# Seven of eight experts' weights fetched at the start, three of them into the attention's query and key tiles

## The chip, the cores and the metric

The kernel runs on one core of a Trainium2 chip. The metric is the time of one execution on the device in microseconds (us). The core has a tensor engine (PE in the profile; PEld are its weight loads), a vector engine (DVE), a scalar engine (ACT), GpSimd (POOL) and a sync engine (SP). Each works through its own queue of instructions in order. SP issues most of the transfers from DRAM to the on-chip memory, and POOL issues the indirect ones, in which a table of row numbers says where each row goes. A transfer runs by itself once it is issued, on 16 DMA engines.

## What is computed

Two layers on 2048 tokens of 128 channels in float32. The first has a mixture of eight experts, attention with 16 heads, and the same mixture once more; the second has a channel mix, a gated long convolution and the channel mix again. The part that matters here is the mixture:

```python
def _L0_ffn_ref(s, W_in, in_norm_w, Wr, expert_bias, Wg, Wu, Wd, enorm_w, out_norm_w, W_out):
    h = rmsnorm(x @ W_in.T, in_norm_w)
    logits = h @ Wr.T
    _, idx = jax.lax.top_k(logits + expert_bias, TOP_K)          # 2 of 8 experts for each token
    gates = ...                                                  # softmax over the two chosen logits
    for e in range(Wg.shape[0]):
        gate = jax.nn.silu(h @ Wg[e].T)
        up = h @ Wu[e].T
        oe = rmsnorm(gate * up @ Wd[e].T, enorm_w[e])
        out = out + gates[:, e:e + 1] * oe
    s_hat = rmsnorm(out, out_norm_w) @ W_out.T

x = x + 0.5 * _L0_ffn_ref(_layernorm(x), ...)
x = x + _L0_attn_ref(_layernorm(x), ...)
x = x + 0.5 * _L0_ffn_ref(_layernorm(x), ...)
```

Each expert has three matrices of 128 x 512. Together with its norm weights they make 1664 numbers in each of 128 partitions (WALL), 832 KB.

## The kernel before

**Dispatch.** The tokens come in 16 tiles of 128, four to a part (EARLY). `dispatch` normalises a part, takes its two best experts for each token and computes the token's place in the list of that expert in DRAM (`hss`). POOL then writes the rows there, one indirect transfer for each tile and choice (L470). The four parts are staggered, so the scatters of one part run beside the arithmetic of the next.

**Blocks.** An expert works on blocks of rows from its list. A general block (numbers below NT = 24) holds 256 rows (15 of them, NPAIR) or 128 (9, NSING). Which expert and which rows it has is only known at run time: `table` computes that on DVE in steps, and SP reads the result into registers before it can issue the fetches.

**Early blocks.** Eight blocks, one for each expert (numbers NT to NT + 7), take the first 128 rows of that expert's list. They need no table and don't wait for the whole dispatch, only for the first six tiles (LEAD). `leading` sets them up. Their rows are fetched by `read` (L550) once the scatters of these six tiles have landed. They go into tiles that attention will later use for its values (`vs`, 512 x 4 floats a partition each). Their outputs go there too. Where an expert has fewer than 128 rows by then, masks make the block's output go nowhere, and the general blocks cover these rows.

**Order of the work.** In `experts`, `work` runs over the early blocks, then over TURNS. Turn i does on the tensor engine: the gate product of block i (`pg`, L732), the transposition of the next block's rows (`pht`, L719), the up product (`pu`, L732) and the down product of the block before (`py`, L755). Between `up` and `down` stands a piece of other work, among them the steps of the table: the last and longest (`named` with `bounded`, L632 to L664) is the piece of turn 4. `down` ends with the square sums on ACT (L772), the product with the norm weights on DVE (L773) and the scatter of the output rows on POOL (L779). Each of `py` and `pht` has one PSUM bank (tags `sb` and `sa`). After `down`, SP is given the fetches of turn i + 3: `fetch_rows` (L713) and `fetch_weights` (L705, and L527 for an early block).

**Weights.** All weight tiles come from one pool with four buffers (tag `w`). Before the dispatch begins, `first_experts` issues the fetches of experts 0 to 3 (L527). Expert 4's fetch is issued in turn 1, after the down product of expert 0 has released its buffer, and so on: expert e + 4 after expert e. A fetch waits in SP's queue until DVE has done the L773 of the block that used the buffer last, and what stands behind it in SP's queue waits as well.

**The zero fill.** Behind each list there must be rows of zeros. `zeros` writes them with one indirect transfer on POOL (L506) whose source is `blank`, the first 16 * ROW = 2064 columns of the first query and key tile, cleared by DVE at the very start (L949).

**The query and key tiles.** `qks` are two tiles of 4096 floats a partition, queries in the first half and keys in the second. Until attention they are only used as said. Pieces of turns 14 to 17 clear the query halves and set the key halves on POOL (L962, L966).

Of the kernel before, what the change touches and what calls it, by code (L numbers as in the profile page):

```python
# [10 lines left out]
F32 = mybir.dt.float32  # L11
# [5 lines left out]
P = 128  # L17
# [15 lines left out]
ROW = D + 1  # L33
# [5 lines left out]
NT = NPAIR + NSING  # L39
# [19 lines left out]
WALL = 3 * DFF + D  # L59
# [14 lines left out]
def macaron_kernel(ctx: ExitStack, tc: tile.TileContext, a: dict, out: bass.AP):  # L74
# [11 lines left out]
    def bank(name, tag=None):  # L86

        if tag is None or tag == "side":
            tags = ("sa", "sb", "px", "py", "pz") if tag is None else turn["side"]
            tag = tags[turn["bank"] % len(tags)]  # L90
            turn["bank"] += 1
        if tag[0] == "p":
            return bank_pair(name, tag)[:, 0, :]
        return psum.tile([P, 512], F32, tag=tag, name=name)
# [90 lines left out]
    def both(*pieces):  # L185
        def run():
            for piece in pieces:
                piece()

        return run  # L190
# [301 lines left out]
    def counts(f):  # L492
        pc = bank(f"pcnt_{f}", "sb")[:, 0:E]
        nc.tensor.matmul(pc, ones, ahead[:, NCH * TPC, :], start=True, stop=True)
        return pc

    def zeros(pc, mp):


        at = mp.tile([P, E], F32, tag="zat", name="zat", bufs=1)  # L500
        nc.vector.tensor_mul(at, pc, owner)
        row = mp.tile([P, 1], F32, tag="zsum", name="zsum", bufs=1)
        nc.vector.tensor_reduce(row, at, AX.X, ALU.add)
        word = mp.tile([P, 1], I32, tag="zword", name="zword", bufs=1)
        nc.vector.scalar_tensor_tensor(word, row, float(ROW), zrow, ALU.mult, ALU.add)
        ins = nc.gpsimd.indirect_dma_start(  # L506
            out=hss[0].rearrange("n w -> (n w)").unsqueeze(1),
            out_offset=bass.IndirectOffsetOnAxis(ap=word, axis=0),
            in_=blank[0],
            in_offset=None,  # L510
        )
        tc.declare_no_dep(ins.ins, group="hs0", reason="rows of their own")
        tc.add_to_no_dep_group("hs0", ins.ins)
        tc.declare_no_dep(ins.ins, group="lead", reason="full blocks, or not used")
        tc.keep_in_program_order(ins)

    def leading(gp, mp, rows, yrows):

        lead = {"w": {}, "hst": {}, "yrow": {}}
        flags = gp.tile([P, 3, E], F32, tag="lflags", name="lflags", bufs=1)  # L520
        masks = gp.tile([P, 3, E], I32, tag="lmasks", name="lmasks", bufs=1)
        idx = gp.tile([P, E], I32, tag="lidx", name="lidx", bufs=1)
        lead["taken"], lead["base"], lead["masks"], lead["idx"] = flags[:, 0], flags[:, 1], masks, idx

        def weights(e):
            lead["w"][NT + e] = mp.tile([P, WALL], F32, tag="w", name=f"w_lead_{e}", bufs=4)
            nc.sync.dma_start(lead["w"][NT + e], a["wall"][e, :, :])  # L527

        def flagged():


            pc = bank("plead", "sb")[:, 0:E]
            nc.tensor.matmul(pc, ones, ahead[:, LEAD, :], start=True, stop=True)
            full = float(P)
            nc.vector.scalar_tensor_tensor(flags[:, 2], pc, full, base, ALU.is_ge, ALU.mult)
            nc.vector.tensor_scalar(masks[:, 2], flags[:, 2], 1.0, None, ALU.max)
            nc.vector.tensor_scalar(flags[:, 0], pc, full, full, ALU.is_ge, ALU.mult)
            nc.vector.tensor_scalar(masks[:, 0], pc, full, float(FAR - 1), ALU.is_ge, ALU.mult)
            nc.vector.tensor_scalar(masks[:, 1], pc, full, float(FAR), ALU.is_lt, ALU.mult)
            nc.vector.tensor_add(flags[:, 1], flags[:, 0], base)  # L540

        def read():
            SP = mybir.EngineType.SP
            first = [
                nc.values_load(masks[0:1, 2, e : e + 1], engines=[SP], min_val=1, max_val=HS_ROWS - TT)
                for e in range(E)
            ]
            for e, row in enumerate(first):
                hst = rows[:, e * ROW : e * ROW + ROW].unsqueeze(1)
                ins = nc.sync.dma_start(  # L550
                    hst, hss[0][bass.ds(row, P), :].rearrange("(s p) c -> p s c", p=P)
                )
                tc.add_to_no_dep_group("lead", ins.ins)
                lead["hst"][NT + e] = hst
                lead["yrow"][NT + e] = yrows[:, e * ROW : e * ROW + ROW].unsqueeze(1)

        return lead, weights, flagged, read

    def table(f, pc, mp, lead=None, scratch=None):
# [115 lines left out]
    def weigh_up(f, mp):  # L675

        g = mp.tile([P, NCH * TPC, 2], F32, tag="gates", name=f"gates_{f}", bufs=1)
        mx = mp.tile([P, NCH * TPC], F32, tag="gmx", name=f"gmx_{f}", bufs=1)
        nc.vector.tensor_reduce(mx, lsel, AX.X, ALU.max)
        nc.vector.tensor_sub(g, lsel, bc_last(mx, 2))  # L680
        nc.scalar.activation(g, g, AF.Exp)
        nc.vector.tensor_reduce(mx, g, AX.X, ALU.add)
        nc.vector.reciprocal(mx, mx)
        nc.vector.tensor_mul(g, g, bc_last(mx, 2))
        return g
# [204 lines left out]
    def stagger(chunks, lag):  # L890

        n = len(chunks[0])
        for s in range(lag * (len(chunks) - 1) + n):
            for c, stages in enumerate(chunks):
                if 0 <= s - lag * c < n:
                    stages[s - lag * c]()
# [1 line left out]

    def first_experts(parts, gp, pieces, heads_):

        with tc.tile_pool(name="moe0", bufs=2, reuse_waits="tile") as mp:
            flat = [t.rearrange("p t h d -> p (t h d)") for t in heads_]
            lead, lead["weights"], flagged, read = leading(gp, mp, *flat)
            for e in range(4):
                lead["weights"](e)
            found = {}

            def counted():  # L910
                found["pc"] = counts(0)
                zeros(found["pc"], gp)

            i = LEAD // TPC
            parts[i][-2] = both(parts[i][-2], flagged)
            rows = parts[i][-1]
            parts[i][-1] = both(
                partial(rows, range(LEAD % TPC)), read, partial(rows, range(LEAD % TPC, TPC))
            )
            decays = decay_pieces()  # L920
            parts[-1][4] = both(parts[-1][4], decays[0])
            parts[-1][-1] = both(counted, parts[-1][-1])
            stagger(parts, 4)
            tab, far, steps = table(0, found["pc"], gp, lead, flat[0][:, E * ROW :])
            steps[0]()
            steps = [*steps[1:5], both(*steps[5:7])]
            steps += [lambda: None] * (E - len(steps))
            experts(0, tab, far, y2s[0], mp, steps + pieces, lead)
        return weigh_up(0, gp), decays[1:]
# [15 lines left out]
    def heads(hp):  # L945
        qks = [hp.tile([P, 2, 4, CT], F32, tag=f"qk{i}", name=f"qk{i}") for i in range(2)]
# [3 lines left out]
        vs = [hp.tile([P, TPC, H, 32], F32, tag=f"v{i}", name=f"v{i}") for i in range(2)]  # L950
# [398 lines left out]
                    for step in places_[s, "b"]:  # L1349
                        step()  # L1350

        return constant_pieces, attention, vs


    def tail(gates, y2):
# [223 lines left out]
    with tc.manual_schedule(engines={EN.PE, EN.DVE, EN.Activation, EN.SP}):  # L1579
        with tc.tile_pool(name="rows0", bufs=2) as gp:  # L1580
            with tc.tile_pool(name="heads", bufs=1, reuse_waits="tile") as hp:
                constant_pieces, attention, vs = heads(hp)
                fold_in()
                parts = [[*dispatch(0, i, EARLY, gp)] for i in range(len(EARLY))]
                early = filter_pieces()
                idle = [fold_out, fold_mu, *constant_pieces()]
                idle += [lambda: None] * (len(early) - len(idle))
                gates, decays = first_experts(parts, gp, [both(*two) for two in zip(early, idle)], vs)
                mixed = combined(0, gates, y2s[0], gp)
                attention(mixed, [dispatch(1, i, LATE, gp) for i in range(len(LATE))], decays)  # L1590
            gates = second_experts(gp)
            banks.close()
            tail(gates, y2s[1])
# [137 lines left out]
```

## Time and profile before

| | us |
|---|---|
| median of three runs | 597.49 (595.13 to 599.95) |
| the profiled execution | 594.65 |
| its span, first to last instruction | 592.9 |

| stretch of the profile, us | what runs | tensor engine busy, us | mean clock granted to it | DMA share |
|---|---|---|---|---|
| 0 to 16 | constants, inputs, four weight fetches; dispatch of the first part | 10.07 of 16 | 0.93 | 0.85 |
| 16 to 41.5 | the rest of the dispatch | 10.10 of 25.5 | 0.50 | 0.42 |
| 41.5 to 53.5 | early blocks of experts 0 to 3 | 11.96 of 12 | 0.87 | 0.36 |
| 53.5 to 66 | early blocks of experts 4 and 5, and the start of 6 | 7.70 of 12.5 | 0.86 | 0.99 |
| 66 to 72 | early blocks of experts 6 and 7 | 5.74 of 6 | 1.00 | 0.89 |
| 72 to 158 | general blocks | 82.11 of 86 | 1.00 | 0.58 |
| 158 to 375 | combination, attention, second dispatch | 193.97 of 217 | 0.99 | 0.27 |
| 375 to 470 | second mixture | 88.83 of 95 | 0.98 | 0.70 |

The rest of the span is the combination and the second layer. The clock is that which the throttle granted, as a share of full speed. The DMA share is the mean busy share of the 16 DMA engines. Over the whole span the tensor engine is busy for 519.3 us (88%), DVE for 356.6, ACT for 272.7 and POOL for 193.3.

A line of the timeline gives the start in us, the duration, the engine, the line of the kernel, the operation and its tiles, and in brackets the time that the engine sat idle before it with what ended the wait. A number of instructions (x8) can be merged in one line.

### The profile page before, as it was taken

What the parts mean: (1) busy time and instruction counts of PE and PEld (TensorE: products, weight loads), DVE (VectorE), ACT (ScalarE), POOL (GpSimd) and SP (SyncE); (2) the same over time, 40 slices, a digit from 0 to 9 for tenths busy, and PEclk for the clock granted to TensorE, in tenths of its full rate; (3) what the DMA queues carried; (4) which work ended last, traced back from release to release, by engine and by line L of the source; (5) the groups of instructions that cost most, each with busy time, mean ns of one, the idle gap of its engine ahead of it and who ended that gap; (6) DMA issues with size and microseconds to landing.
All of it is one profiled execution on the core that took longest, in us unless ns stands there. A gap on an engine that the chain in (4) does not pass through costs nothing. (4 is left out here: it accounts for less than half of the span.)

```text
span 592.9 us, 11265 instructions
## 1 busy us (share of the span) xinstructions
PE 519.3 (88%) x3921; PEld 397.7 (67%) x3921; DVE 356.6 (60%) x1114; ACT 272.7 (46%) x669; POOL 193.3 (33%) x201
## 2 busy tenths in 40 slices
PE   5458899999779989998898888699999989789996
PEld 5347898898536555565465554379999974568874
DVE  5766454564335766767778866634444432868775
ACT  4563232223334556566766654123233223884365
POOL 0677445753331201011003447313333335420110
PEclk9559899999999999999999999999999999989999
DMA  8536956666040355064030001368767725000002
GB/s 303 204 86 205 317 202 217 176 202 211 24 108 28 46 146 212 1 190 170 25 48 20 28 28 46 113 207 246 231 208 237 228 76 144 2 1 1 0 2 71
DMA packets 37598, 74.30 MB, mean 125 GB/s; under 512 B 4571, under 2 KB 26882, under 8 KB 36256
## 3 DMA queue, kind: packets, MB, share of 16 engines
q1 hardware_dynamic: 33040, 64.00, 35.4%
q0 software_dynamic: 4496, 9.52, 4.6%
q8 instruction: 33, 0.54, 0.4%
q14 instruction: 29, 0.24, 0.1%
HBM read 52.66 MB, written 21.38 MB: 125 GB/s over the span
## 5 line engine op out<-in xcount | busy, mean ns | idle before, releaser
L779 POOL DMA_INDIRECT y<-yrow_f,idx_f x64 | 62.9, 984 | 106.5 <-issue 56.6
L1160 ACT ACTIVATE es<-ps 128x1024 f32<-128x1024 f32 x64 | 65.3, 1021 | 52.5 <-PE ps L1123 30.9
L1143 DVE TENSOR_REDUCE m<-pm 128x4 f32<-128x1024 f32 x64 | 77.5, 1220 | 12.3 <-PE pm L1106 12.3
L1123 PE MATMUL ps<-qa,qk 32*128 32x256 f32 x512 | 72.7, 401 | 11.9 <-ACT es L1160 9.6
L470 POOL DMA_INDIRECT hs<-hrow,posi_f x64 | 61.8, 965 | 53.9 <-issue 23.9
L748 DVE TENSOR_TENSOR hg_f<-pu_f,sg_f 128x1024 f32<-128x1024 f32 (+1 forms) x45 | 45.5, 1011 | 51.0 <-PE pu_f L732 51.0
L1106 PE MATMUL pm<-qk 32*128 32x256 f32 x512 | 73.2, 400 | 0.6 <-ACT qk L1053 0.6
L732 PE MATMUL pg_f<-ht_f,w_f 128*128 128x256 f32 (+1 forms) x296 | 63.6, 359 | 3.0 <-DMA w_f<-in_wall_dram 1.6
L755 PE MATMUL py_f<-w_f,hg_f 128*128 128x128 f32 x512 | 63.8, 276 | 2.0 <-DVE idx_f L776 1.2
L755 PEld LDWEIGHTS py_f<-w_f,hg_f 128*128 128x128 f32 x512 | 61.7, 192 | 3.7 <-DVE yrow_f L773 2.3
L772 ACT ACTIVATE ysq_f<-py_f 128x128 f32<-128x128 f32 x72 | 19.4, 274 | 96.9 <-PE py_f L755 89.1
L1123 PEld LDWEIGHTS ps<-qa,qk 32*128 32x128 f32 x512 | 43.6, 184 | 30.0 <-ACT es L1160 22.4
L741 ACT ACTIVATE sg_f<-pg_f 128x1024 f32<-128x1024 f32 (+1 forms) x45 | 38.4, 853 | 53.3 <-PE pg_f L732 51.7
L732 PE MATMUL pu_f<-ht_f,w_f 128*128 128x256 f32 (+1 forms) x296 | 61.7, 351 | 0.0
L732 PEld LDWEIGHTS pg_f<-ht_f,w_f 128*128 128x128 f32 x296 | 49.7, 194 | 8.5 <-DVE hg_f L748 2.2
L732 PEld LDWEIGHTS pu_f<-ht_f,w_f 128*128 128x128 f32 x296 | 48.7, 191 | 5.0
L1106 PEld LDWEIGHTS pm<-qk 32*128 32x128 f32 x512 | 44.5, 184 | 2.5 <-issue 1.5
L773 DVE TENSOR_TENSOR yrow_f<-py_f,w_f 128x256 f32<-128x256 f32 (+1 forms) x37 | 14.4, 389 | 38.0 <-ACT ysq_f L772 38.0
L1170 PE MATMUL po<-es,v 128*32 128x256 f32 x512 | 34.9, 391 | 0.0
L171 POOL TENSOR_TENSOR cf_f<-cf_f,mhalf 128x8 f32<-128x8 f32 (+1 forms) x9 | 13.5, 1502 | 64.3 <-DVE cf_f L844 63.5
L724 DVE TENSOR_SCALAR ht_f<-pht_f,pack 128x256 f32<-128x256 f32 (+1 forms) x37 | 16.5, 446 | 23.7 <-PE pht_f L719 23.7
L1155 DVE TENSOR_TENSOR qa<-pmt,qk 128x256 f32<-128x256 f32 x32 | 13.5, 422 | 25.8 <-PE pmt L1149 24.3
(306 smaller groups left out, 926.4 us busy)
## 6 DMA issues: line engine op xcount, KB each, us to landing
w_f<-in_wall_dram SPq DMA_DIRECT2D x36, 832.0 KB, 4.9
hs<-blank SPq DMA_DIRECT2D x8, 1032.0 KB, 15.1
w_lead<-in_wall_dram SPq DMA_DIRECT2D x8, 832.0 KB, 7.8
y_f<-y SPq DMA_DIRECT2D x14, 258.0 KB, 5.0
hst_f<-hs SPq DMA_DIRECT2D x27, 129.0 KB, 3.0
pack<-in_pack_dram SPq DMA_DIRECT2D x1, 1729.0 KB, 8.6
heads<-qkc SPq DMA_DIRECT2D x3, 512.0 KB, 2.6
qk<-heads SPq DMA_DIRECT2D x12, 128.0 KB
```

What stands on the lines that cost most here:

```text
L470: ins = nc.gpsimd.indirect_dma_start(out=hss[f], out_offset=bass.IndirectOffsetOnAxis(ap=st["posi"][:, t, k : k + 1], axis=0), in_=hrow[:, ...
L732: nc.tensor.matmul(ph[:, k, :], w[t][:, o + k * P : o + k * P + P], ht[t], start=True, stop=True)
L741: nc.scalar.activation(sg, pg, AF.Silu)
L748: nc.vector.tensor_mul(hg[t], pu, sg)
L755: nc.tensor.matmul(py[:, s, :], hg[t][:, k, ts(s, P)], w[t][:, 2 * DFF + k * D : 2 * DFF + k * D + D], start=(k == 0), stop=(k == NFC - 1),)
L772: nc.scalar.activation(sq[:, s], py[:, s], AF.Square, accum_out=yrow[:, s, D : D + 1])
L779: ins = nc.gpsimd.indirect_dma_start(out=y2, out_offset=bass.IndirectOffsetOnAxis(ap=idx[:, s : s + 1], axis=0), in_=yrow[:, s, :], in_off ...
L1106: nc.tensor.matmul(sc[:, jj, i, :], qs[c][r, g, col + i * P : col + (i + 1) * P], ks[c][r, g, col : col + S], start=True, stop=True,)
L1123: nc.tensor.matmul(sc[:, jj, i, :], ks[c][r, g, col + i * P : col + (i + 1) * P], tops[s][r, :], start=True, stop=True,)
L1143: nc.vector.tensor_reduce(m, sc, AX.X, ALU.max, negate=True)
L1160: nc.scalar.activation(es, sc, AF.Exp, scale=scale)
L1170: nc.tensor.matmul(po[32 * j : 32 * j + 32, :], vs[c][:, (b % 2) * 2 + i, (g % 2) * (H // 2) + (g // 2) * 4 + j, :], ess[s, j // 2][:, j % ...
```

## The change

The weights of the early blocks get places of their own for three experts: expert 0 and expert 1 in the second query and key tile, one behind the other (2 x 1664 of its 4096 columns), and expert 2 in the first, behind the 2064 columns that hold the zeros. The four buffers of the pool then hold experts 3 to 6. Seven fetches are issued before the dispatch and not four. Expert 7 takes the buffer that expert 3 releases, in turn 4 as before, and the general blocks follow as before.

```diff
-    def leading(gp, mp, rows, yrows):
+    def leading(gp, mp, homes, rows, yrows):
...
         def weights(e):
-            lead["w"][NT + e] = mp.tile([P, WALL], F32, tag="w", name=f"w_lead_{e}", bufs=4)
+            if e in homes:
+                lead["w"][NT + e] = homes[e]
+            else:
+                lead["w"][NT + e] = mp.tile([P, WALL], F32, tag="w", name=f"w_lead_{e}", bufs=4)
             nc.sync.dma_start(lead["w"][NT + e], a["wall"][e, :, :])
...
-    def first_experts(parts, gp, pieces, heads_):
+    def first_experts(parts, gp, pieces, qks, vs):
...
-            flat = [t.rearrange("p t h d -> p (t h d)") for t in heads_]
-            lead, lead["weights"], flagged, read = leading(gp, mp, *flat)
-            for e in range(4):
+            wide = [t.rearrange("p i g s -> p (i g s)") for t in qks]
+            flat = [t.rearrange("p t h d -> p (t h d)") for t in vs]
+            homes = {0: wide[1][:, 0:WALL], 1: wide[1][:, WALL : 2 * WALL]}
+            homes[2] = wide[0][:, 16 * ROW : 16 * ROW + WALL]
+            lead, lead["weights"], flagged, read = leading(gp, mp, homes, *flat)
+            for e in range(7):
                 lead["weights"](e)
...
-        return constant_pieces, attention, vs
+        return constant_pieces, attention, qks, vs
...
-                constant_pieces, attention, vs = heads(hp)
+                constant_pieces, attention, qks, vs = heads(hp)
...
-                gates, decays = first_experts(parts, gp, [both(*two) for two in zip(early, idle)], vs)
+                gates, decays = first_experts(parts, gp, [both(*two) for two in zip(early, idle)], qks, vs)
```

## The prediction

> **What bounds the kernel now.** The page's second part comes first, to find stages in which the engines are starved:
>
> ```profile
> span 592.9 us, 11265 instructions
> ...
> PEclk9559899999999999999999999999999999989999
> DMA  8536956666040355064030001368767725000002
> ```
>
> A slice is 14.8 us. DMA is busy in slice 0, falls to 5 and 3 tenths in slices 1 and 2, and stands at 9 in slice 4 (59 to 74 us), just where the granted clock dips to 8: the transfers are bunched, and TensorE is waiting beside them. The chain of waits doesn't reach so far back (it begins at 374 us), so the stage of the eight early blocks is read from the timeline of TensorE, 50 to 72 us (these are lines of one answer; every left-hand number is a start):
>
> ```profile
> 55.52 1.13 PE L732 MATMUL pg_f<-ht_f,w_lead 128*128 128x128 f32 x8 [2.03 <-DMA w_lead<-in_wall_dram]
> ...
> 61.33 1.77 PE L732 MATMUL pg_f<-ht_f,w_lead 128*128 128x128 f32 x8 [2.78 <-DMA w_lead<-in_wall_dram]
> ...
> 65.82 1.06 PE L732 MATMUL pg_f<-ht_f,w_lead 128*128 128x128 f32 x8
> ...
> 68.61 1.06 PE L732 MATMUL pg_f<-ht_f,w_lead 128*128 128x128 f32 x8
> ...
> 71.93 1.97 PE L732 MATMUL pg_f<-ht_f,w_f 128*128 128x256 f32 x8 [0.26 <-DMA w_f<-in_wall_dram]
> ```
>
> These are the gate products of early experts 4, 5, 6 and 7, and of the first block of the table (t0). Experts 4 and 5 wait for weights. An undisturbed early block takes 2.79 us from gate to gate (65.82 to 68.61); the block begun at 61.33 takes 4.49. From 72 to 156 us TensorE is busy 82.1 of 84 us with no wait above 0.8 us, at clock 1.00: whatever t0 gains is carried through that stage. What else must be ready for t0 stands in the other queues:
>
> ```profile
> 58.28 0.96 POOL L470 DMA_INDIRECT hs<-hrow,posi_f  x1 [0.30 <-issue]
> ...
> 58.37 0.17 DVE L632 CAST tab_tab<-tab_has 128x24 int32<-128x24 f32 x1
> ...
> 61.62 0.28 DVE L773 TENSOR_TENSOR v<-py_f,w_lead 128x128 f32<-128x128 f32 x1
> ...
> 61.96 0.33 SPq L527 DMA_DIRECT2D w_lead<-in_wall_dram  x1
> ...
> 64.71 0.40 SPq L713 DMA_DIRECT2D hst_f<-hs  x1
> 66.84 0.35 SPq L705 DMA_DIRECT2D w_f<-in_wall_dram  x1
> ```
>
> 58.28 is the last scatter of rows. VectorE works on the table from 58.37 to 61.62 (3.25 us), and only then evacuates expert 3's output; that frees the buffer for expert 7's weights, issued at 61.96. Behind it in SP's queue stand the rows and the weights of t0. And DMA by stage:
>
> ```profile
> core 0: us, PE busy (x) PEld busy (x) DVE busy (x) ACT busy (x) POOL busy (x), PEclk, DMA share, GB/s
> 5.00:20.00 15.00, 7.20 (x39) 6.02 (x37) 9.71 (x56) 7.90 (x31) 2.03 (x2) 0.79 1.01 397
> ...
> 22.00:34.00 12.00, 6.24 (x27) 5.57 (x26) 9.03 (x56) 6.46 (x26) 9.24 (x10) 0.50 0.16 53
> 54.00:62.00 8.00, 3.70 (x29) 3.57 (x30) 4.78 (x22) 1.22 (x4) 5.19 (x7) 0.98 1.02 378
> ```
>
> The engines of the DMA are nearly empty from 22 to 34 us and full from 54 to 62.
>
> **The change, part by part.** No work is added or removed: eight fetches of 832 KB before and after. Three of them (experts 4, 5, 6) move from 49.36, 51.8 and 54.7 us to directly behind the first four, and the weights of experts 0 to 2 land in the qk tiles.
>
> *Three more issues at the start.* The four stand at 5.4, 6.0, 6.8 and 7.6, about 0.75 us apart; three more keep SP until 10.3. SP's next work is at 30.0 (loads of row numbers), so 20 us of slack hide them. Data: 2.56 MB at the 397 GB/s of the row 5 to 20 is 6.4 us, so the last weights land at some 28 us instead of 21. First to need them is expert 4 at 53.3: hidden by 25 us. The row fetches of L550, from 34.2, come 6 us behind.
>
> *Beside them POOL's scatters (L470, from 17.7).* Landing time is 2.4 to 2.7 us in the window 17 to 25, where weights still stream until about 21; it is 9.1 to 9.8 in the window 48 to 53, where POOL has also sent the zero fill (L506: 128 rows of 2064 words, 1.06 MB) into its own queue. Between these ends I take 2.7, from the nearer case. The Trainium skill ("DMA: Bandwidth & Descriptors", "Queues, rings and completion order") has each DMA engine take turns between queues by packet, which would speak for the low end; POOL kept its pace of 1.26 us per scatter even at 9.8. Cost 0; the other end is a rival below.
>
> *Homes.* The zero fill reads columns 0 to 2063 of the first qk tile; home 2 begins at 2064. The memsets and copies of qk come at 107.5 to 125 us on POOL, 50 us after experts 0 to 2 are done. Other addresses for TensorE to read: no row shows a price; between a small gain and a small loss I take 0. If the cover of 50 us were gone, POOL's queue would stop at 107.5.
>
> *Waits removed.* Without them expert 4 starts at 50.54 + 2.79 = 53.33 (2.19 earlier), expert 5 not 5.81 but 2.79 later (3.02 more), and the slow block is worth 4.49 - 2.79 = 1.70. Together 6.91: expert 7 would be due at 61.70.
>
> *What is late next.* First, VectorE. With expert 4's product done 2.2 us earlier the table work begins at about 56.1 and ends at 59.4; the evacuation of expert 3 ends at 59.65. Expert 4's down product needs the same PSUM bank (tag sb, one buffer), so TensorE, done at about 58.0, stands 1.7 us; expert 6's gate is at 60.6, and expert 7 is ready at 63.4. Second, expert 7's own weights, the one fetch not moved: issue follows the evacuation, so 59.7 (against 61.96). Its landing time was 5.9 us with the other fetches still draining; the 36 later fetches of the same size have a median of 4.9 in a calmer queue; I take 4.9. It lands at 64.6: a wait of 1.2. The skill's same page ("Anatomy of one DMA") gives 2.0 us and bytes by 436 GB/s for a transfer issued by GpSimd, an estimate of 3.95 us here, and the sum below would be 5.2 instead of 4.2; the trace has the very transfer, so its row is taken. Queued behind it on SP are t0's rows: the gap from 61.96 to 64.71 contains 1.2 us for the scatters to land, so 1.55 without it: 61.3, or at 59.24 + 2.4 = 61.6 when the last scatter is down; then t0's weights 1.2 us later (the spacing of such pairs, as at 104.30 and 105.50): 62.8, landed at 67.7.
>
> *Clock.* The wait of 2.03 left the clock at 1.00, that of 2.78 was followed by 0.62 in the window 62 to 66. "TensorE: Matmul & The Clock Gate" (Part 1) wants an idle window of some 3.4 us before the clock halves; the trace dropped after less, with a short stall before. The rule gives no drop for stalls of 1.7 and 1.2, and so does the row of 2.03; the row of 2.78 would, if short stalls add up, and then 1.7 of the gain is lost (2.5 left). I take no drop.
>
> *Sum.* Expert 7 at 64.6 against 68.61; t0's gate follows 3.32 - 0.26 = 3.06 later at 67.7, which is also when its weights land. 71.93 - 67.7 = 4.2 us. The profiled execution took 594.65 (span 592.9): 590.4 after. The three timed runs have median 597.49 (595.13 to 599.95), the profiled one lies at their low edge; the same 4.2 off the median is 593.3.
>
> **The rivals.**
>
> *A, the above,* 591.5 to 595.5. For it: each remaining term is a queue position that the trace shows.
>
> *B, more than that.* If expert 7's and t0's weights land in 3.95 us, or SP's chain is tighter than I read it, t0 comes at 66.0 to 66.8: a gain of 5.2 to 6. Bounded by 6.9. Time 591 to 592. Against it: the median of 4.9 over 36 fetches.
>
> *C, the transfer only trades places.* The last scatter's landing stays where it was (SP saw it at about 64.7): it hangs on the zero fill ahead of it in POOL's queue and not on the weights. Then t0's rows go at 64.7, its weights at 65.9, and t0 starts at 70.8: a gain of 1.1, time 596.4. For it: the late landings begin with the fill at 49.4. Against: 1.06 MB should be gone by 54, and the queue stayed full of weights until 62.
>
> *D, slower: the scatters starve in the prologue.* With weights streaming until 28, the first eight scatters could land only then, as those at 48 to 53 did; if POOL may run no further ahead, it stops at 18 to 28 us. Everything in its queue slips: the last scatter, t0's rows. Slack is 4.2 us (t0 then starts as before); one such landing, 9.5, costs 5.3 beyond that: 602.8, and a second one would make it 612. Against it: the pace of 1.26 held at the same landing times, and 2.7 was seen beside weights.
>
> *E, it does nothing:* the fetches could be held back by waits on the qk tiles. The only earlier writer is the memset at 1.39 to 3.17 us, so this is negligible and counted with C.
>
> **How the numbers follow.** A 0.58, B 0.14, C with E 0.14, D 0.14. The predicted time is A's, 593.3. About 1% (6 us) is what a measurement of this kernel can tell from no change. Faster by more: most of B (0.12) and the edge of A (0.07), with the spread of the runs: 0.19. Slower by more, above 603.5: the worse part of D and what I have not seen, 0.09. Within: 0.72. The range reaches from B's low end less a part of the run spread, 589, to C plus it, 600; outside lie about 0.1 of D and a little of the rest. A's own range is 591.5 to 595.5.
>
> **What would show it.** Right: no wait of experts 4 and 5 on weights; a stall of TensorE near 58 us behind VectorE's table work; a wait of 1 to 2 us for expert 7's weights; those issued at about 59.7; t0's gate near 67.7 at clock 1.00; scatters still 1.26 us apart. Wrong: t0's rows fetched as late as 64 (C), gaps among the scatters from 18 to 28 us (D), a half clock at 62 to 66, or a stage from t0's gate to the last down product that is longer than the 84 us of 72 to 156.

## The result and the profile after

| | before | after |
|---|---|---|
| median, us | 598.64 (594.92 to 601.92, 14 runs) | 593.36 (591.55 to 595.76, 14 runs) |
| ratio after / before | | 0.9921 (95% interval 0.9899 to 0.9944) |
| the profiled execution, us | 594.65 | 593.90 |
| its span, us | 592.9 | 592.1 |

The ratio makes 4.7 us (3.4 to 6.0); the two medians lie 5.3 us apart. The two profiled executions are only 0.75 us apart, because that of before was one of its shortest. So the spans can't be set against each other: the stage has to be read, and for before a second profile is needed (it comes with the last experiment below).

The page of after, its rows by slices of 14.8 us:

```profile
span 592.1 us, 11259 instructions
...
PEclk9559999999799999999999999799999998989999
DMA  8933846766041264073020001467767715000002
```

The second DMA digit (15 to 30 us) went from 5 to 9: the three more fetches. The fourth and fifth (44 to 74 us) went from 6 and 9 to 3 and 8. The clock's dip to 8 in the fifth slice is gone. In its place stand a 7 at 148 to 163 us and one at 370 to 385 us, where before has 9: half clock fell into other places in this execution (the four warming matmuls at 157 us took 3.33 us, against 1.74). So this pair of spans doesn't show all that the stage gained.

TensorE's timeline in the stage of the early blocks: the gate products of experts 4 and 5, the down product of expert 4, the gates of experts 6 and 7 and of the first block of the table, t0. The line numbers of `experts` have moved by 4.

```profile
54.58 1.06 PE L736 MATMUL pg_f<-ht_f,w_lead 128*128 128x128 f32 x8
...
57.37 1.06 PE L736 MATMUL pg_f<-ht_f,w_lead 128*128 128x128 f32 x8
...
60.98 1.16 PE L759 MATMUL py_f<-w_lead,hg_f 128*128 128x128 f32 x8 [1.55 <-DVE v L777]
61.97 1.06 PE L736 MATMUL pg_f<-ht_f,w_lead 128*128 128x128 f32 x8
...
66.59 1.13 PE L736 MATMUL pg_f<-ht_f,w_lead 128*128 128x128 f32 x8 [1.67 <-DMA w_lead<-in_wall_dram]
...
70.06 1.97 PE L736 MATMUL pg_f<-ht_f,w_f 128*128 128x256 f32 x8 [0.34 <-DMA w_f<-in_wall_dram]
```

Experts 4 and 5 wait for nothing; both waits of 2.03 and 2.78 us are gone. Two others have taken their place, 1.55 us behind VectorE and 1.67 us for the one set of weights that is still fetched late. The products after both stalls take their full-clock time (1.06 to 1.16 us), so the clock didn't drop. The other queues at that place, all engines in one answer:

```profile
57.35 0.17 DVE L636 CAST tab_tab<-tab_has 128x24 int32<-128x24 f32 x1
...
58.47 0.96 POOL L470 DMA_INDIRECT hs<-hrow,posi_f  x1 [0.30 <-DVE v L640]
...
60.64 0.28 DVE L777 TENSOR_TENSOR v<-py_f,w_lead 128x128 f32<-128x128 f32 x1
...
60.98 0.34 SPq L531 DMA_DIRECT2D w_lead<-in_wall_dram  x1
62.21 0.38 SPq L717 DMA_DIRECT2D hst_f<-hs  x1
...
63.93 0.35 SPq L709 DMA_DIRECT2D w_f<-in_wall_dram  x1
```

The table work runs from 57.35 to 60.6 us; behind it VectorE evacuates expert 3's output, and only that lets TensorE's down product and SP's fetch of expert 7's weights go, both at 60.98. The rows of t0 follow 1.2 us behind, its weights 1.7 us behind those. Last, DMA by stage (the columns are those of the table shown of before):

```profile
core 0: us, PE busy (x) PEld busy (x) DVE busy (x) ACT busy (x) POOL busy (x), PEclk, DMA share, GB/s
...
22.00:34.00 12.00, 6.43 (x28) 5.76 (x27) 8.99 (x56) 6.46 (x26) 9.26 (x10) 0.50 0.59 229
...
54.00:62.00 8.00, 6.45 (x58) 6.26 (x57) 6.83 (x28) 2.45 (x8) 6.17 (x7) 1.00 0.23 65
```

The transfers have moved from the full stretch (54 to 62 us: share 1.02 before, 0.23 now) to the empty one (22 to 34 us: 0.16 before, 0.59 now), and TensorE works 6.45 of these 8 us and not 3.70.

### The profile page after: what moved, and what is told of

The parts are those of the page before. It is cut to its first block, busy times and chain, and to the rows that moved or that the text cites. A ratio compares the mean times of both kernels' runs of the same rounds, so it can differ in the third digit from the quotient of the medians.

```text
span 592.1 us, 11259 instructions
## 1 busy us (share of the span) xinstructions
PE 520.3 (88%) x3921; PEld 399.8 (68%) x3921; DVE 356.5 (60%) x1114; ACT 272.8 (46%) x669; POOL 193.1 (33%) x201
```

## The experiments

The theory: the gain is that experts 4 and 5 no longer wait for weights, and what is left is set by the queue of VectorE's table work, expert 7's fetch, t0's rows and t0's weights. The rivals: the prologue pays for the three fetches (scatters starve), the late landing of the scatters sets t0's rows anyway, or the gain is TensorE's clock more than the waits. A run tells them apart in two ways: its time, and the start of t0's gate, from which the rest of the program follows. The expectations call the runs by the short names that stand in brackets here.

**One fetch ahead and not three (e1).** Only expert 0 gets a place of its own, so that expert 4's weights are fetched at the start and those of 5 to 7 late.

```diff
-            homes = {0: wide[1][:, 0:WALL], 1: wide[1][:, WALL : 2 * WALL]}
-            homes[2] = wide[0][:, 16 * ROW : 16 * ROW + WALL]
+            homes = {0: wide[1][:, 0:WALL]}
...
-            for e in range(7):
+            for e in range(5):
```

> Only expert 0 gets a home, five fetches are issued at the start: expert 4's wait goes, experts 5 to 7 are fetched when buffers come free, as before. Theory (queues): expert 4's start sets the table work on VectorE and with it the issue of expert 7's weights, so most of the gain comes from this one fetch: 3 to 4.5 us under before, ratio 0.9925 to 0.995; expert 5 still waits 1 to 2 us for its weights. Rival (the waits add up one by one): a gain in proportion to the wait removed, 2.0 of 4.8 us, ratio 0.9965 or nearer to 1. Rival (only the clock gains): the wait of expert 5 grows to 4 us or more and the clock still drops: ratio 1.

594.74 us (592.29 to 596.39), before 598.30 on that chip, ratio 0.9943 (0.9921 to 0.9965), which is 3.4 us. TensorE's timeline, the gate of expert 5, its up product and t0's gate, then SP's fetches for experts 5 and 7 and for t0's rows:

```profile
58.60 1.76 PE L736 MATMUL pg_f<-ht_f,w_lead 128*128 128x128 f32 x8 [2.18 <-DMA w_lead<-in_wall_dram]
...
60.36 1.92 PE L736 MATMUL pu_f<-ht_f,w_lead 128*128 128x128 f32 x8
...
70.89 1.97 PE L736 MATMUL pg_f<-ht_f,w_f 128*128 128x256 f32 x8 [1.17 <-DMA w_f<-in_wall_dram]
```

```profile
51.88 0.34 SPq L531 DMA_DIRECT2D w_lead<-in_wall_dram  x1
...
59.90 0.33 SPq L531 DMA_DIRECT2D w_lead<-in_wall_dram  x1
62.26 0.40 SPq L717 DMA_DIRECT2D hst_f<-hs  x1
```

Expert 4's wait is gone, that of expert 5 stays (2.18 us against 2.78), and its products (1.76, 1.92) fall to half clock. Still t0 starts at 70.89, only 0.8 us later than with three fetches ahead. The first of the late fetches is worth about 3.4 of the 4.7 us (2.1 to 4.7; the share that the first rival gave it, about 2, lies at the edge). Experts 5 and 6 are asked for no earlier than before (51.88 and 54.87 us against 51.78 and 54.73), as their buffers come free with experts 1 and 2. But with expert 4's transfer no longer ahead of them their weights take less time: expert 6's landed after 6.3 us and not 9.8, and expert 5's gate starts 6.7 us after its fetch and not 9.6. And with expert 4 on time, VectorE's table work and the evacuation behind it come earlier, so that expert 7's weights go out at 59.90 and not at 61.96, and t0's rows at 62.26 and not at 64.71. The other two fetches together bring 1.3 us by the points; the intervals overlap.

**All eight ahead (e2).** Expert 7's weights go, in two pieces, to an attention tile that is free until then and to what is left of the second query and key tile. No fetch of the early blocks is late now.

```diff
+            homes[7] = TwoParts(ms[0].rearrange("p i h d -> p (i h d)"), wide[1][:, 2 * WALL :])
...
-            for e in range(7):
+            for e in range(8):
...
+            if e == 7 and e in homes:
+                nc.sync.dma_start(homes[e].a, a["wall"][e, :, 0 : 2 * DFF])
+                nc.sync.dma_start(homes[e].b[:, 0 : WALL - 2 * DFF], a["wall"][e, :, 2 * DFF : WALL])
+                return
```

> The changed kernel with expert 7's weights fetched at the start too, in two pieces, to one of attention's m tiles and the rest of the second qk tile. Theory: the wait of 1.7 us for expert 7 goes, and the first general block's rows and weights are no longer queued behind that fetch: its gate comes 1 to 2 us earlier than in the changed kernel, ratio to before 0.988 to 0.991; the next bound is the landing of the last scatter (rows fetched at 61.5 to 62.5). Rival (rows hang on the scatters alone): no wait of expert 7 but a longer one for the first general block, ratio as the changed kernel, 0.992.

591.87 us (590.40 to 594.07), ratio 0.9898 (0.9863 to 0.9933), 6.1 us. All engines in one answer (SP's two fetches are those for t0):

```profile
60.69 0.38 SPq L733 DMA_DIRECT2D hst_f<-hs  x1
...
61.08 1.16 PE L775 MATMUL py_f<-w_lead,hg_f 128*128 128x128 f32 x8 [1.51 <-DVE v L793]
...
62.43 0.35 SPq L725 DMA_DIRECT2D w_f<-in_wall_dram  x1
...
64.87 1.06 PE L752 MATMUL pg_f<-ht_f,m 128*128 128x128 f32 x8
```

The wait of 1.67 us for expert 7's weights is gone (64.87), the stall behind VectorE stays, and t0's rows and weights go out 1.5 us earlier. t0's gate is at 68.85, 1.2 us earlier than in the changed kernel, and 6.4 us after its weights were asked for. This is the fastest version of the study by its median; its interval overlaps that of the changed kernel, so the 1.4 us between the two ratios are not shown. SP waited 0.9 us for the scatters here and got the rows at 60.69: the last scatter, sent at 58.37, had landed some 2.3 us later.

**The table's last step behind the evacuation (e3).** In turn 4 the down product of the block before comes ahead of the table's last step, so that neither TensorE nor the fetch of expert 7's weights stands behind it.

```diff
+                late = i == 4 and i < len(pieces)
-                if i < len(pieces):
+                if i < len(pieces) and not late:
                     pieces[i]()
                 if i > 0:
                     down(turns[i - 1])
+                if late:
+                    pieces[i]()
```

> The changed kernel with one exchange: in turn 4 the down product of expert 3 and its evacuation come before the last step of the table on VectorE. Theory: the stall of 1.55 us of TensorE behind the table goes or shrinks below 0.5, expert 7's weights are issued about 3 us earlier (near 57.5) and nobody waits for them; the first general block then hangs on the rows' scatters and its own weights, 1 to 2 us earlier than in the changed kernel: ratio to before 0.988 to 0.991. Rival (the table is needed first): its rows wait for the later table, ratio 0.992 or above.

595.47 us (591.96 to 598.79), ratio 0.9948 (0.9928 to 0.9969): not faster than the changed kernel. The expectation failed, though its first half came true: expert 4's down product no longer stalls (one of 0.41 us comes at the next, behind the moved table work), and expert 7's weights were asked for at 58.45 and not 60.98. SP's waits from 58 to 72 us (us in total, times, longest) show what came instead:

```profile
SPq L717 <- DMA hs<-hrow,posi_f: 3.1, 1, 3.1
```

and TensorE's timeline what it did to t0, its rows first, then its gate:

```profile
66.35 0.44 PE L723 MATMUL pht_f<-ident,hst_f 128*128 128x128 f32 x2 [1.38 <-DMA hst_f<-hs]
...
70.56 3.22 PE L736 MATMUL pg_f<-ht_f,w_f 128*128 128x256 f32 x8 [1.98 <-DMA w_f<-in_wall_dram]
```

SP waited 3.1 us for the last scatters and sent for t0's rows only at 64.00; all that was won went into waits for rows and weights, with a half clock on top (3.22 against 1.97). The new theory was that the 832 KB of expert 7, now in flight beside the last scatters, hold up their landing.

**Both edits together (e8, e10)** settle that: with expert 7's weights fetched at the start, nothing large is in flight at 58 us, and the table's step is as late as in the run before. It ran twice, the first time on a chip where the kernel before takes 620 us (more on that below).

> e2 and e3 together: expert 7's weights at the start and the table's last step behind the evacuation. In e3 SP waited 3.1 us for scatters to land, with expert 7's weights in flight beside them. Theory: without that transfer the scatters land by 61, rows go out at 61 to 62 and the first general block starts at 68 to 69.5: ratio as e2, 0.989 to 0.991. Rival (the later table is what delayed e3): rows at 63.5 or later here too, ratio 0.993 or above.

There 616.29 us, ratio 0.9943 (0.9925 to 0.9961). And again on a chip like the first:

> e8 once more, on a chip like that of e1 to e4. Theory (e3 lost because expert 7's weights delayed the landing of the last scatters): without that transfer the rows go out at 61 to 62 and the first general block starts at 68 to 69.5: ratio 0.988 to 0.991. Rival (the later table delayed e3): rows at 63.5 or later, ratio 0.993 or above.

593.04 us (591.32 to 595.10), before 598.16, ratio 0.9921 (0.9897 to 0.9945). The rows of t0 go out without a wait for scatters, at

```profile
60.88 0.38 SPq L733 DMA_DIRECT2D hst_f<-hs  x1
...
67.93 1.97 PE L752 MATMUL pg_f<-ht_f,w_f 128*128 128x256 f32 x8 [1.13 <-DVE lidx L797]
```

With the same late table step, the rows go at 60.88 without expert 7's transfer and at 64.00 with it. So it is that transfer that delayed them, and not the later table. t0's gate is at 67.93, the earliest of the runs on chips of 598 us, but the time was expected at 0.988 to 0.991 and is 0.9921: the interval reaches there, the point doesn't. The exchange of the two steps brings nothing that these runs can measure beyond eight fetches alone.

**The three fetches behind the row fetches (e4).** They are issued at 38 us, after the scatters of the first six tiles have landed, so that the prologue is as before.

```diff
-            for e in range(7):
+            for e in range(4):
...
-                partial(rows, range(LEAD % TPC)), read, partial(rows, range(LEAD % TPC, TPC))
+                partial(rows, range(LEAD % TPC)), read, *[partial(lead["weights"], e) for e in (4, 5, 6)],
+                partial(rows, range(LEAD % TPC, TPC)),
```

> The changed kernel with the three extra fetches (experts 4 to 6) issued not at the start but behind the row fetches, from about 38 us. Theory: only landing before 53 us counts; the weights land at 46 to 48 beside the scatters: same as the changed kernel within 0.5 us, ratio 0.991 to 0.993. Rival (prologue traffic costs the changed kernel something): faster than the changed kernel by 0.5 us or more, with the first early block 0.2 us earlier. Rival (fetches beside the zero fill and scatters cost): slower than the changed kernel by 1 us or more, with gaps among the scatters.

593.38 us (591.24 to 595.76), ratio 0.9919 (0.9894 to 0.9944), the changed kernel's own. TensorE's timeline: the down product of expert 4, the gate of expert 7, t0's gate.

```profile
60.29 1.16 PE L759 MATMUL py_f<-w_lead,hg_f 128*128 128x128 f32 x8 [1.56 <-DVE v L777]
...
65.72 1.13 PE L736 MATMUL pg_f<-ht_f,w_lead 128*128 128x128 f32 x8 [1.48 <-DMA w_lead<-in_wall_dram]
...
70.41 1.96 PE L736 MATMUL pg_f<-ht_f,w_f 128*128 128x256 f32 x8 [1.55 <-DMA w_f<-in_wall_dram]
```

The same two stalls, and the same time. For that it doesn't matter whether the fetches go out in the prologue or at 38 us, as long as the weights are there at some 53 us.

One thing looks like a price of the prologue and, by the traces, isn't one. In the four profiles with seven or eight fetches at the start (the changed kernel, eight ahead, and the two with the table later, on the chips of 598 us) the first scatter is at 17.75 to 17.86 us, and expert 4's gate is due at 54.7 us in the mean. In the four with four or five (this run, one fetch ahead, and two profiles of before) it is 17.27 to 17.66 and 53.7 (for before, 2.79 us behind expert 3's gate). But the difference is there before a fifth fetch is sent, which the changed kernel does at 8.69 us. The first products of the program, in the changed kernel and in this run:

```profile
1.46 4.21 PE L311 MATMUL warm_i<-ident 128*128 128x128 f32 x18 [1.46 <-POOL ident masks.py:199]
...
1.46 3.96 PE L311 MATMUL warm_i<-ident 128*128 128x128 f32 x18 [1.46 <-POOL ident masks.py:199]
```

VectorE's copy behind them (L381) starts at 8.57 and at 8.11 us, and these 0.46 us stay until the first scatter (17.86 and 17.41). Up to that copy both programs have sent the same transfers. What differs is the clock: its first rise is on record at 6.00 us in the changed kernel and at 5.02 here. After the dispatch it comes up again 40.96 us later in both, at 46.96 and 45.98. In all eight profiles this second rise lies between 44.56 (before, first profile) and 47.37 us (eight ahead), and expert 4's gate is due between 53.33 and 54.73 us in the same order, profile by profile. Why the clock is late in just the four with more fetches stays open; their traffic can't be the reason for a difference that was there before it. The rival's earlier first block came (41.29 us against 41.74), but it brought no time here: TensorE waits 1.55 us for t0's weights and not 0.34, as they went out at 63.28, 0.65 us earlier, and were there no earlier.

**The kernel before, looked at again (e5).** A second profile of it, meant for the clock, fell on another chip.

> The kernel before once more, for a second profile: the profiled execution shown (594.65 us) lies at the low edge of its runs (median 598). Theory: the same waits of experts 4 and 5, and more time at half clock than in the profile shown, in the stage of 54 to 72 us or at another place where TensorE stands still; the first general block at 72 us or later. Rival (the spread comes from elsewhere): the early blocks as in the profile shown within 0.5 us, and the excess in a later stage.

619.45 us, and the kernel before takes 620.17 there (616.51 to 624.13, 59 runs). Its waits from 0 to 75 us:

```profile
DVE hg_f L748 <- remote: 13.8, 1, 13.8
ACT sg_f L741 <- remote: 10.9, 1, 10.9
```

VectorE and ScalarE stand still for 11 to 14 us by causes that the profile puts outside the program's own instructions, and expert 0's gate is at 52.99 us and not at 41.5. The fetches of experts 4 and 5 then have the time they lacked: what is left of these waits is some 1 us. On such a chip the mechanism of the change is hardly in play, and runs there say little about it. Why the engines stand still there stays open.

**The clock by itself (e6, e11).** Useless matmuls ahead of the gates of experts 4 and 5 in the kernel before, to fill the waits and keep the clock up.

```diff
             for i, t in enumerate(turns):
+                if lead and i in (4, 5):
+                    tag = ("px", "py", "pz")[turn["pair"] % 3]
+                    keep_warm(bank_pair(f"warm_l{i}", tag)[:, 0, :], 16 if i == 5 else 12)
                 sg = gate(t)
```

> The kernel before with matmuls of no use in the two waits: 12 x 128 columns ahead of expert 4's gate, 16 x 128 ahead of expert 5's (1.3 and 1.7 us at full clock, less than the waits of 2.0 and 2.8). Theory: the clock stays at 1.00, the 1.70 us of slow products after the second wait go, the waits for weights stay: 1 to 3 us under before, ratio 0.995 to 0.998. Rival (the slow stretch costs nothing, as the first general block waits for its own weights anyway): ratio 1 within 0.001.

622.16 us, ratio 1.0042 (1.0025 to 1.0059); and a second time:

> e6 once more, on a chip like that of e1 to e4. Theory: with TensorE kept at work in most of the two waits the clock stays at 1.00 through 54 to 72 us, the waits for weights themselves stay (experts 4 and 5 start when their weights land), the products behind them run at full speed: 1 to 3 us under before, ratio 0.995 to 0.998. In e6 it was slower there, 1.004. Rival (the slow products cost nothing, since the next start waits for a transfer anyway, and the added matmuls get in the way): ratio 1.000 or above.

621.18 us, ratio 1.0035 (1.0017 to 1.0053). Both fell on the chips of 620 us (before: 620.17 and 619.32). There are no waits of 2 us to fill there, so the added matmuls push the products back and cost 2.2 to 2.6 us. They were also twice as long as planned: 2.74 and 3.60 us at a clock of 1.00 in the second profile, more than the waits of 2.03 and 2.78 us that they were meant to fit in. What the clock alone is worth on the other chips was not measured.

**t0's weights ahead of its rows (e7, e12).** On top of eight fetches, SP gets t0's weights first, since they land last.

```diff
-                    fetch_rows(turns[i + 3])
-                    fetch_weights(turns[i + 3])
+                    two = (fetch_rows, fetch_weights)
+                    for fetch in two[::-1] if i == 5 and len(pieces) else two:
+                        fetch(turns[i + 3])
```

> As e2, and the first general block's weights are asked for ahead of its rows. Theory: its weights then don't stand behind the wait for the scatters, are issued about 1.3 us earlier, near 61.0, and the block starts 0.5 to 1.5 us earlier than in e2 (68.85 there): ratio to before 0.987 to 0.989. Rival (the transfer meets the last scatters in flight and delays the rows): rows fetched at 63 or later, TensorE waits for them, ratio 0.991 or above.

618.49 us, ratio 0.9971 (0.9953 to 0.9988); and again:

> e7 once more, on a chip like that of e1 to e4: eight fetches ahead, and the first general block's weights asked for before its rows. Theory: its weights are issued near 61.0 instead of 62.4, the block starts at 67.5 to 68.3 instead of 68.85: ratio 0.987 to 0.990. Rival (the transfer meets the last scatters in flight and delays the rows, as in e3): rows at 63 or later, TensorE waits for them, ratio 0.991 or above.

617.11 us, ratio 0.9960 (0.9942 to 0.9978). Again both on chips of 620 us. Against the run of eight fetches with the later table step there (0.9943), it isn't better; against eight fetches alone it was compared nowhere, and on a chip of 598 us it wasn't tried.

**The kernel before, a typical execution (e9).** The last profile fell on a chip like the first.

> The kernel before once more (e5 fell on a chip on which it takes 620 us and VectorE and ScalarE stand still for many us in the dispatch). Theory: the waits of experts 4 and 5 again, with more time at half clock in the stage of 54 to 72 us than in the profile first shown; the first general block at 72 to 75 us. Rival (the spread of the runs comes from elsewhere): the early blocks within 0.5 us of the profile first shown, the excess in a later stage.

598.86 us, 0.7 above the median of 598.16 there, with a span of 597.1. TensorE's timeline: gate and up product of expert 4, the gates of 5 and 7, t0's gate; VectorE's evacuation of expert 3 and SP's fetch of t0's rows stand among them.

```profile
56.93 2.04 PE L732 MATMUL pg_f<-ht_f,w_lead 128*128 128x128 f32 x8 [2.85 <-DMA w_lead<-in_wall_dram]
...
58.98 1.91 PE L732 MATMUL pu_f<-ht_f,w_lead 128*128 128x128 f32 x8
...
62.40 1.41 PE L732 MATMUL pg_f<-ht_f,w_lead 128*128 128x128 f32 x8
...
64.86 0.28 DVE L773 TENSOR_TENSOR v<-py_f,w_lead 128x128 f32<-128x128 f32 x1
...
66.84 0.40 SPq L713 DMA_DIRECT2D hst_f<-hs  x1
...
70.53 1.13 PE L732 MATMUL pg_f<-ht_f,w_lead 128*128 128x128 f32 x8 [1.39 <-DMA w_lead<-in_wall_dram]
```

Here the half clock comes behind the first wait already: expert 4's block takes 5.47 us from gate to gate (56.93 to 62.40) and not 2.79. That isn't all of its price. Its up product ends late, behind it VectorE's table work, and behind that the evacuation of expert 3: 64.86 against 61.62 in the first profile. Of these 3.24 us 1.41 are expert 4's later start (56.93 against 55.52), and the other 1.8 its two slow products. So expert 7's weights and t0's rows are asked for late too (rows 66.84 against 64.71), expert 7 has a wait of its own, and t0's gate is at 74.67. That is 2.7 us later than in the first profile of before, and 4.6 us later than in the profile of after (70.06), while the time of the two kernels differs by 4.7.

Why the clock fell behind the first wait here and behind the second in the first profile can be read from the clock's records. In all fourteen traces each stretch at one clock, up to the last that the end cuts off, lasts a whole multiple of 3.41 us. So the clock changes only at steps of 3.41 us, and these lie differently against the program in each execution. Below are steps of three profiles: before's first, before's last, and after. Behind the comma stands TensorE's busy time in the step; PEclk is the clock that was granted.

```profile
core 0: us, PE busy (x) PEld busy (x) DVE busy (x) ACT busy (x) POOL busy (x), PEclk, DMA share, GB/s
51.39:54.80 3.41, 2.10 (x19) 1.91 (x18) 2.54 (x14) 1.22 (x4) 2.50 (x4) 1.00 0.89 287
...
58.21:61.63 3.42, 0.64 (x7) 0.48 (x6) 3.11 (x16) 0.37 (x2) 1.95 (x2) 1.00 0.96 364
61.63:65.04 3.41, 3.41 (x19) 3.41 (x18) 0.55 (x4) 0.85 (x2) 2.60 (x3) 0.50 0.96 291
...
52.88:56.29 3.41, 1.21 (x11) 1.01 (x10) 2.12 (x9) 0.57 (x3) 2.68 (x3) 1.00 1.01 400
56.29:59.71 3.42, 2.78 (x13) 2.81 (x14) 0.00 (x0) 0.70 (x2) 2.51 (x4) 0.50 0.97 346
...
64.02:67.44 3.42, 1.75 (x16) 1.59 (x15) 1.21 (x4) 0.37 (x2) 2.35 (x3) 1.00 1.00 374
67.44:70.85 3.41, 3.07 (x25) 2.83 (x24) 1.69 (x5) 0.96 (x3) 0.20 (x1) 1.00 1.03 344
```

In this stage, half clock followed steps at full clock in which TensorE worked for 0.64, 1.21, 1.24 (one fetch ahead) and 1.43 us (table later), and did not follow those of 1.75 us and more. The wait of 2.03 us in the first profile is split, 1.3 us in one step and 0.7 in the next; of the 2.85 us here, 2.2 lie in one step. Over the whole spans the border lies near half of a step as well, but less sharply: steps 43 to 50% busy are found on both sides, and a few falls came after busier ones.

All profiles of these chips side by side, worked out from their timelines and spans:

| kernel | t0's gate, us | span, us | span less t0's gate, us |
|---|---|---|---|
| before, first profile | 71.93 | 592.9 | 521.0 |
| before, last profile | 74.67 | 597.1 | 522.4 |
| changed kernel | 70.06 | 592.1 | 522.0 |
| one fetch ahead | 70.89 | 593.0 | 522.1 |
| three fetches at 38 us | 70.41 | 591.8 | 521.4 |
| eight ahead | 68.85 | 591.8 | 523.0 |
| three ahead, table later | 70.56 | 595.2 | 524.6 |
| eight ahead, table later | 67.93 | 589.5 | 521.6 |

The last column varies by 3.6 us and doesn't follow the first: in these profiles what the rest of the program takes shows no dependence on when t0 starts. It also shows how far one span can mislead about 2 us.

## Why the prediction held, step by step

**The time.** 593.3 was predicted and 593.36 measured, by the case A that was called likeliest: waits removed, new and shorter stalls in their place, the rest of the gain carried to the end. That the two agree to 0.1 us is luck. The base was a median of 597.49 us, which more runs put at 598.64, and two errors inside the sum cancel (below).

**Waits removed.** As predicted, no wait is left at experts 4 and 5. The undisturbed 2.79 us from gate to gate hold (54.58 to 57.37).

**What is late next.** The stall behind the table work was put at 1.7 us and is 1.55, at the bank `sb` and the evacuation that were named. The wait for expert 7's weights was put at 1.2 and is 1.67. Taking away the fetch took away this wait and let the others go earlier (eight ahead), and with the table work no longer in front of the evacuation the stall at that product was gone; so both causes are shown.

**A size that was too small: the landings.** 4.9 us were taken for expert 7's weights and for t0's. They took 5.5 and about 6.1 (63.93 to 70.0). Other fetches follow 1.1 to 1.7 us behind each; that these slow them is likely and wasn't measured by itself. This put t0 back by 1.2 us in its last landing alone.

**The homes.** Products that read their weights from the query and key tiles take 1.06 us, like those that read them from the pool: the cost of 0 held.

**A start that was too early: expert 4 at 53.33.** The three issues cost nothing that the traces show: SP had its slack, and the rows of the early blocks are fetched at 34.24 us (34.21 before). But expert 4 comes at 54.58 us. The 53.33 was worked out from the one profile in which the clock came up earliest of all eight (44.56 us, against 46.96 in the profile of after), and expert 4's gate follows that rise. So 1.25 us were missing from the sum before the first wait. Together with the landings t0 is at 70.06 and not at 67.7.

**What made up for both: the clock before the change.** The sum gave the slow block 1.70 us, from a profile in which the clock fell behind the second wait. Where it falls behind the first, as in the typical execution, before's t0 comes 2.7 us later. The predicted step of t0's gate, 4.2 us, was reached as 74.67 less 70.06, 4.6 us, with two errors of 2.4 and 2.7 us that cancel by luck. The size of the second rests on one typical profile.

**The clock after the change.** No drop was predicted for stalls of 1.7 and 1.2 us; none came at 1.55 and 1.67. The step of the clock with the least work in this stage still had 1.75 us of it.

**The rivals.** B, faster by shorter landings, fell with the landings of 5.5 and 6.1.

C, late scatters, doesn't hold here: SP sent for t0's rows at 62.21, right behind the fetch in front of them and without a wait for scatters. It put the late landings down to the zero fill alone. The fill is sent as before (49.64 us, 49.44 before), yet a scatter behind it landed after 4.9 us and not after 9.1 to 9.8, so the weights had their share. The mechanism itself exists, as the later table showed: 832 KB sent at the same moment made SP wait 3.1 us for the scatters.

D, starved scatters in the prologue, came true by half. The scatters sent from 19.33 to 20.59 us landed after 5.7 to 5.9 us and not after the 2.7 that was taken. That figure had been misread: it belongs to scatters sent at 20.40 and 21.66 us, when the weights were nearly through (DMA share 0.22 from 21 to 22 us). But POOL kept its pace of 1.26 us from 19.33 to 29.43, as before, and the three fetches at 38 us gave the same time: the cost was 0 although the landings doubled.

**What stays open.** How much of the gain is the clock's and how much the waits' own (the runs meant for it fell on chips where the waits don't occur, and their matmuls were longer than the waits); why the clock came up late in the four profiles with seven or eight fetches at the start; whether t0's weights ahead of its rows would help; whether eight ahead beats the changed kernel, 0.9898 against 0.9921 with intervals that overlap.

## What to carry to other kernels

Where a chain of buffers is refilled just in time, the gain need not grow with the number of fetches moved: putting the first late one ahead of time brought most of what three brought, as the transfers behind it landed sooner and the work that releases later buffers began sooner. A fetch moved earlier can also land on another transfer that is about to be needed; ask what else is in flight at its new place before calling it hidden. And where the clock falls behind some stalls and not behind others, one profile of the kernel before can be off by more than half of what the change is worth (2.7 of 4.7 us here): take a second one whose time is near the median. Before putting a delay down to some transfers, see whether it is there before they begin.

## What the chip showed that was not expected

- The clock changed only at steps of 3.41 us, which lie differently in each execution, and in this stage it fell after steps in which TensorE worked for 1.43 us or less and not after those of 1.75 us or more. So the length of a stall alone doesn't tell: a wait of 1.98 us (table later) was followed by half clock and one of 2.03 us (before, first) was not.
- The price of half clock was not only slower products: through VectorE's queue two slow products (1.8 us) held up the fetch of the next weights and rows, and a further wait of 1.39 us came of it.
- Small scatters beside bulk fetches landed after 5.7 to 5.9 us (changed kernel, 19 to 21 us) and cost nothing: SP fetched the early rows at 34.24 us, 34.21 before.
- One 832 KB fetch issued together with the last small scatters put the rows behind them from 60.88 to 64.00 us.
- On two other chips the same program takes 620 us and not 598, with stalls of VectorE and ScalarE in the dispatch, and the one gain measured on both kinds is smaller there by the points (eight ahead with the table later: 0.9943 there, 0.9921 here; the intervals overlap).
